# Nine products a job on VectorE, earlier rows of B, and the norm ahead of the gates, in the Mamba layer of a four-layer stack

## The chip, the cores and the metric

The kernel runs on one core of one Trainium2 chip. The metric is the device time of one execution in microseconds (us); smaller is better. Engine names in the profile are PE (TensorE matmul), PEld (TensorE weight load), DVE (VectorE), ACT (ScalarE), POOL (GpSimd) and SP (SyncE, which here issues the DMAs).

## The reference, cut to what matters

Four layers follow each other on a float32 image batch of shape (8, 192, 56, 56), each of the form x + layer(group_norm(x)). Layer 0 is an involution. Layers 1, 2 and 3 are state-space (Mamba) layers. Layer 1, the one that the change is about, cuts the 192 normed channels into three slices of 64 and runs the same Mamba block on each:

```python
xn = layer_norm(group_norm(x))                   # over the 192 channels
for xs in three slices of 64 channels:
    xi, z = xs @ in_proj.T                       # 512 inner channels each
    xc = silu(causal_conv4(xi))
    dt, B, C = split(xc @ x_proj.T)              # 4, 16, 16
    dt = softplus(dt @ dt_proj.T + bias)
    h = h * exp(dt * A) + (dt * xc) * B          # 16 states per channel, along the tokens
    y = (sum over states of h * C) + xc * D
    out = (y * silu(z)) @ out_proj.T + xs
x = x + layer_norm(out of all three) @ proj.T + proj_b
```

Layers 2 and 3 do the same once for all channels, with 384 inner channels.

## The kernel before, in words

**Tiles.** An image has 3136 tokens, cut into 7 chunks of 448 (T). A chunk of layer 1 gives three jobs, one for each slice of 64 channels, called the slice 0, slice 1 and slice 2 job here; 8 images x 7 chunks x 3 slices are 168 jobs. A job has 512 inner channels in nd = 4 groups of 128, and each group has 16 states. A unit treats 4 states of one group: 128 partitions hold 32 channels x 4 states, and the free dimension holds 4 blocks of channels x 448 tokens. So a job of layer 1 has 16 units, numbered 0 to 15, four to a group; q is the number of a unit within its group. Layers 2 and 3 have nd = 3 and 12 units a job.

**What a unit needs.** Line numbers are those of the profile of the kernel before.

- `load_ops` (L713) brings delta and delta times x of a whole group from DRAM, each row repeated for four states, into a tile `rep` (two buffers): four DMAs of 448 KB.
- `decays` (L729): ScalarE takes exp(delta A) into one of two PSUM tiles `da`, one for each half of a unit. Two instructions a half.
- `inputs_begin` (L737): ScalarE copies the carried state into column 0 of the unit's tile `uhg` (nine buffers).
- The product, delta x times B, 128 x 1792 elements. Either GpSimd makes it (`inputs_by_pool`, L748), with B from a row tile that a DMA has spread over the partitions (`row_in`, L629), or VectorE does (`inputs_by_vector`, L754), with B from a PSUM tile `b` that one bfloat16 matmul of TensorE has spread (`spread_b`, L723). There is one `b` bank. The set `pool_units` says which: in layer 1 GpSimd has the eight odd units.
- `scan` (L758): VectorE runs the recurrence, in two halves of 128 x 898. A half needs its decays and the product.
- `keep` (L762): ScalarE copies the last state out. It is the "carry" of the profile.
- `readout` (L767): GpSimd multiplies with C, in place, for every unit, once `keep` is done.
- `reduce` (L773, L776): TensorE sums the states into a PSUM tile `y` (one bank). The first matmul of a group (L773) starts that bank anew and must wait until the group before has been taken out by `gated` (L792), a VectorE product at the head of the units with q = 3.
- `nothing` (L782): matmuls with zeros, which change no result.

**The order is written out by hand.** Engines take their instructions in program order. At unit k the program issues: row loads; `gated`; `reduce(k-3)`; first half of the background; first half `scan(k,0)`; `decays(k+1,0)`; `inputs_begin(k+3)`; GpSimd's product of unit k+2; `readout(k-2)`; VectorE's product of unit k+1; `spread_b(k+2)`; second half of the background; `scan(k,1)`; `keep(k)`; `decays(k+1,1)`.

**The background** prepares the next job while a job runs. It is a list of steps, dealt out by `places` over 32 places (two a unit) in six stretches (`bounds`): convolutions (L1026, evicted at L593); at place 6, that is unit 3, one switch of ScalarE's table for the silus (L596, L577; table back at L569), with the output projection of the job before (L1054, L1056, evicted at L1061); x_proj (L601, evicted at L605), the splitting of B into bfloat16 parts (L612, L613, evicted at L617) and the deltas (L635, evicted at L640); at place 14 (unit 7) or 18 (unit 9) a second switch for the softplus (L643); then delta times x (L647 on TensorE, L650 on VectorE) and its stores; and last the gates (L1044, evicted at L674). A step's cost is a number written at the step. In the slice 0 job the projection and second norm of the chunk before come ahead of the gates. The slice 1 job also holds, behind the gates, the norm of the next chunk: group norm (L330), mean (L537), centring on VectorE (L543), square, variance, scaling (L554), affine (L559), and then eight DMAs (L991) that put the slices into a tile `xs`. The convolutions of the next chunk's first slice read `xs` at the start of the slice 2 job. The softplus switch is at place 14 in the slice 0 job and at place 18 in the other two.

Of the kernel before, what the change touches and what calls it, by code (L numbers as in the profile page):

```python
# [49 lines left out]
def pause(cost=1.0):  # L50
    return Step(None, lambda: None, 9, cost)
# [35 lines left out]
def conv_mamba_stack(ctx: ExitStack, tc: tile.TileContext, a, out):  # L87
# [583 lines left out]
    def evict(w, dst, src, m):  # L671

        if w.inb is None:
            nc.scalar.copy(dst, src)  # L674
        else:
            nc.scalar.activation(dst, src, AF.Identity, bias=w.inb[:, m : m + 1])  # L676

    def gate_steps(pool, w, u, z_mm, z_cost):

        zps = {}  # L680

        def gate(j):
            zps[j] = z_mm(j)

        def gate_out(j):
            if j == 0:
                u.zs = pool.tile([128, w.nd, T], F32, tag="zs", name="zs", bufs=2)
            evict(w, u.zs[:, j, :], zps[j][:, :T], w.nd + j)

        return [Step(lambda j=j: gate(j), lambda j=j: gate_out(j), 1, z_cost) for j in range(w.nd)] + [pause(0.5)]  # L690

    def ssm_layer(pool, w, jobs, n_slots):


        nd = w.nd
        units = [(i, j, q) for i in range(len(jobs)) for j in range(nd) for q in range(NQ)]
        groups = [(i, j) for i in range(len(jobs)) for j in range(nd)]
        per_job = nd * NQ
        pool_units = {1, 3, 5, 7, 9, 11, 13, 15} if nd == 4 else {1, 3, 6, 7, 9, 11}
        pool_rows = sorted({m % NQ for m in pool_units})  # L700
        us = [Layer() for _ in jobs]
        carry = []
        for s in range(n_slots):
# [1 line left out]
        reps, brow, uhg, ys = {}, {}, {}, {}  # L705
# [8 lines left out]
                    out=t[:, r].rearrange("p c t -> p (c t)"), in_=src.unsqueeze(1).to_broadcast([32, 4, 2 * T])  # L714
                )

        def spread_b(k):

            if k in by_pool:
                return  # L720
            i, j, q = units[k]
            brow[k] = banks.b.tile([128, 512], F32, tag="b", name="b")
            nc.tensor.matmul(brow[k][:, :T], lhsT=pick_b[:, q, :], rhs=us[i].parts, start=True, stop=True)  # L723
# [14 lines left out]

        by_pool = {k for k in range(len(units)) if (k % per_job) in pool_units}

        def inputs_by_pool(k):
            if k not in by_pool:
# [5 lines left out]
        def inputs_by_vector(k):  # L750
            if k in by_pool:
                return
            b = brow[k][:, :T].unsqueeze(1).to_broadcast([128, NR, T])
            nc.vector.tensor_mul(uhg[k][:, :, 1:], reps[k // NQ][:, :, 1, :], b)  # L754

        def scan(k, h):
            v = uhg[k][:, 2 * h : 2 * h + 2, :].rearrange("p r t -> p (r t)")
            nc.vector.tensor_tensor_scan(v, banks.da[h][:, 63:961], v, 0.0, ALU.mult, ALU.add)  # L758
# [31 lines left out]
        def gated(g):  # L790
            i, j = groups[g]
            nc.vector.tensor_mul(us[i].zs[:, j, :], us[i].zs[:, j, :], ys[g][:, :T])  # L792

        n_places = 2 * per_job
        def bounds(job):

            silu = 8 if nd == 3 else 6
            softplus = silu + (6 if nd == 3 else 8 if job[0] == 1 else 12)
            return (0, silu), (silu, silu + 2), (silu + 2, softplus), (softplus, softplus + 1), (softplus + 2, softplus + 4), (softplus + 4, n_places)

        def places(*stretches):


# [22 lines left out]
                us[0].row_in(0, q)  # L826
            us[0].row_in(1, q)
        load_ops(0)
        spread_b(0)
        for k in range(3):  # L830
            inputs_begin(k)
        inputs_by_vector(0)
        spread_b(1)
        inputs_by_pool(0)
        inputs_by_pool(1)
        decays(0, 0)
# [2 lines left out]
        n_units = len(units)  # L839
# [7 lines left out]
        for k, (i, j, q) in enumerate(units):  # L847
            m = k % per_job
            if m == 0:

                fetch, outs, rest = tail
                if i + 1 < len(jobs):
                    u = us[i + 1]
                    at = bounds(jobs[i + 1])
                    stretches = *jobs[i + 1][2](u, us[i], outs), rest + jobs[i + 1][3](u)
                    plan = places(*((steps, *p) for steps, p in zip(stretches, at)))
                else:
                    gates = Step(None, lambda: with_gates(lambda: None, us[i]), 0, 0.3, block=True)
                    plan = places(([gates], 4, 6), (outs + rest, 8, n_places))
                plan[3][:0] = [Step(None, fetch, 2, 0.0)]  # L860

            if i + 1 < len(jobs) and m - (per_job - NQ) in pool_rows:
                us[i + 1].row_in(0, m - (per_job - NQ))
            if i and m < NQ:
                us[i].row_in(1, m)
            if k >= NQ + 3 and q == 3:
                gated(k // NQ - 1)
            if k >= 3:
                reduce(k - 3)

            more = 3 - math.ceil(load_of(plan[2 * m] + plan[2 * m + 1]))
            nothing(k - 3, more > 2)
            bg.run(plan[2 * m])
            nothing(k - 3, more > 0)
            load_when_free(k)
            scan(k, 0)
            if k + 1 < n_units:
                decays(k + 1, 0)
            if k + 3 < n_units:
                inputs_begin(k + 3)  # L880
            if k + 2 < n_units:
                inputs_by_pool(k + 2)
            if k >= 2:
                readout(k - 2)
            if k + 1 < n_units:
                inputs_by_vector(k + 1)
            if k + 2 < n_units:
                spread_b(k + 2)
            bg.run(plan[2 * m + 1])
            nothing(k - 3, more > 1)  # L890
            load_when_free(k)
            scan(k, 1)
            keep(k)
            if k + 1 < n_units:
                decays(k + 1, 1)
            if m == per_job - 1:
                tail = jobs[i][4](us[i])
# [67 lines left out]
    def mamba_jobs(pool, w):  # L965
        jobs = []
        chunks = Chunks(pool, 1)
        cks = chunks.all
        for ck in cks:
# [50 lines left out]
            for i in range(3):  # L1020

                def prepare(u, *beside, i=i, ck=ck, norm=norm):
                    def conv_mm(j):
                        pm = mm_tile()
                        for k in range(2):
                            nc.tensor.matmul(  # L1026
                                pm[:, :T], lhsT=w.inconv[:, k, j * 128 : (j + 1) * 128],
                                rhs=ck.xs[:, i, 2 - 2 * k : 2 - 2 * k + T], start=(k == 0), stop=(k == 1),
                            )
                        return pm  # L1030

                    convs, *others, stores = project_steps(pool, w, u, conv_mm, 2, *beside)
                    if i == 0:
                        stores = stores + [Step(None, lambda: chunks.fetch_next(ck), 2)]
                        if ck.place == 0:
                            convs = norm() + convs
                    return convs, *others, stores

                def gates(u, i=i, ck=ck):
                    after_gates = cks[ck.place + 1].norm() if i == 2 and ck.place + 1 < len(cks) else []  # L1040

                    def z_mm(j):
                        pm = mm_tile()
                        nc.tensor.matmul(  # L1044
                            pm[:, :T], lhsT=w.inz[:, j * 128 : (j + 1) * 128], rhs=ck.xs[:64, i, 2 : T + 2], start=True, stop=True
                        )
                        return pm

                    return gate_steps(pool, w, u, z_mm, 1) + after_gates

                def after(u, i=i, ck=ck, finish=finish):
                    def out_proj():
                        u.ps = mm_tile()
                        nc.tensor.matmul(u.ps[:64, :T], lhsT=skip_d, rhs=ck.xs[:64, i, 2 : T + 2], start=True, stop=False)  # L1054
                        for j in range(4):
                            nc.tensor.matmul(u.ps[:64, :T], lhsT=w.outw[:, j, :], rhs=u.zs[:, j, :], start=False, stop=(j == 3))  # L1056

                    def leave():
                        if i == 0:
                            ck.y = pool.tile([64, 3, T], F32, tag="y", name="y")  # L1060
                        nc.scalar.copy(ck.y[:, i, :], u.ps[:64, :T])  # L1061

                    def fetch():
                        if i == 2:
                            chunks.fetch_again(ck)

                    return fetch, [Step(out_proj, leave, 1, 5)], finish() if i == 2 else []

                jobs.append((i, c == 0, prepare, gates, after))
        return jobs  # L1070

# [74 lines left out]
    with ExitStack() as stack:  # L1146
        banks.y = stack.enter_context(tc.tile_pool(name="ps_iy", bufs=1, space=PSUM))
        banks.mm = stack.enter_context(tc.tile_pool(name="ps_im", bufs=6, space=PSUM))
        pool = stack.enter_context(tc.tile_pool(name="inv", bufs=1))
        with tc.manual_schedule():  # L1150
            involution(pool)
    for layer, w in enumerate((w1, w2, w3), 1):
        with ExitStack() as stack:
            scan_banks(stack)
            pool = stack.enter_context(tc.tile_pool(name=f"ssm{layer}", bufs=1))
# [75 lines left out]
```

## Time and profile before

| what | value |
|---|---|
| time, median of 3 runs | 25285.75 us (25262.34 to 25312.53) |
| profiled execution: time and span | 25314.83 us, 25313.0 us |
| share of the span busy: PE, DVE, ACT, POOL | 83%, 89%, 67%, 92% |
| first scan of layer 1, last gating of layer 1 | 1680.36 us, 17363.03 us |
| granted TensorE clock, 2000 to 16000 us | 0.79 of full speed |
| share of DMA engine time, 2000 to 16000 us | 0.36 |

A group of instructions in the profile has its line, engine and operation, what it writes and reads, and its count; behind the first bar stand busy time and mean duration in ns, behind the second the time that the engine was idle just before these instructions, and what it waited for. A line of waits has the waiting engine and line, what it waited for, and total us, times and longest. In a timeline a line has start, duration, engine, line and operation; instructions of one kind that follow each other are merged, and a bracket has the idle time before them with its cause. For TensorE the count of a merged line holds weight loads as well as matmuls.

### The profile page before, as it was taken

What the parts mean: (1) busy time and instruction counts of PE and PEld (TensorE: products, weight loads), DVE (VectorE), ACT (ScalarE), POOL (GpSimd) and SP (SyncE); (2) the same over time, 40 slices, a digit from 0 to 9 for tenths busy, and PEclk for the clock granted to TensorE, in tenths of its full rate; (3) what the DMA queues carried; (4) which work ended last, traced back from release to release, by engine and by line L of the source; (5) the groups of instructions that cost most, each with busy time, mean ns of one, the idle gap of its engine ahead of it and who ended that gap; (6) DMA issues with size and microseconds to landing.
All of it is one profiled execution on the core that took longest, in us unless ns stands there. A gap on an engine that the chain in (4) does not pass through costs nothing.

```text
span 25313.0 us, 232064 instructions
## 1 busy us (share of the span) xinstructions
PE 21123.4 (83%) x71870; PEld 6720.0 (27%) x71870; DVE 22641.3 (89%) x15661; ACT 16946.5 (67%) x32354; POOL 23383.1 (92%) x6772
## 2 busy tenths in 40 slices
PE   9988888888888888888888888888888887888888
PEld 3322222222222222222222222222333332333332
DVE  8879988998899889998998899897999998999998
ACT  1137776767766776766776676676777776777776
POOL 4469999999999999999999999998999998999999
PEclk9988777877777777777777787778888888888888
DMA  4433333333333333333333333333444443444443
GB/s 106 105 101 123 122 119 117 122 121 119 118 122 121 119 120 119 123 119 119 123 119 120 121 120 118 121 119 108 139 141 136 139 140 120 141 138 139 138 145 128
DMA packets 1184872, 3132.61 MB, mean 124 GB/s; under 512 B 163756, under 2 KB 446404, under 8 KB 1183496
## 3 DMA queue, kind: packets, MB, share of 16 engines
q1 hardware_dynamic: 1180824, 3116.70, 37.9%
q8 instruction: 564, 9.24, 0.1%
q14 instruction: 684, 5.60, 0.1%
q10 hardware_dynamic: 2800, 1.06, 0.0%
HBM read 2399.92 MB, written 555.55 MB: 117 GB/s over the span
## 4 chain that ended last, share of the span: by engine, by line
DVE 29%; PE 25%; ACT 19%; issue 11%; POOL 9%; DMA 6%; SPq 2%; DVEq 0%; POOLq 0%; ACTq 0%
DVE uhg L758 20%; ACT da L729 8%; DVE uhg L754 6%; POOL uhg L767 6%; PE y L776 4%; PE mm L635 4%; POOL uhg L748 3%; PE mm L416 3%; DMA rows<-bc 3%; PE y L782 2%; ACT L569 2%; PE y_inv L451 2%; PE y L773 2%; PE mm L612 2%; DMA rep<-ops 2%
## 5 line engine op out<-in xcount | busy, mean ns | idle before, releaser
L758 DVE TENSOR_TENSOR_SCAN uhg<-da,uhg 128x898 f32<-128x898 f32 x8064 | 15928.1, 2011 | 1284.0 <-ACT da L729 1261.9
L767 POOL TENSOR_TENSOR uhg<-uhg,rows 128x1792 f32<-128x1792 f32 x4032 | 14746.3, 3675 | 654.5 <-ACT carry L762 425.9
L729 ACT ACTIVATE da<-rep,k 128x448 f32<-128x448 f32 x16128 | 10255.9, 636 | 1816.6 <-DVE uhg L758 1438.7
L748 POOL TENSOR_TENSOR uhg<-rep,rows 128x1792 f32<-128x1792 f32 x2016 | 8038.2, 3987 | 375.5 <-DMA rep<-ops 206.2
L776 PE MATMUL y<-uhg,k 128*32 128x448 f32 x32256 | 4756.8, 666 | 562.0 <-POOL uhg L767 560.2
L754 DVE TENSOR_TENSOR uhg<-rep,b 128x1792 f32<-128x1792 f32 x2016 | 4031.8, 2000 | 658.9 <-PE b L723 615.1
L762 ACT COPY carry<-uhg 128x4 f32<-128x4 f32 x4032 | 787.3, 195 | 3514.0 <-DVE uhg L758 3464.3
L773 PE MATMUL y<-xc,w_d 128*128 128x448 f32 x2016 | 1522.0, 850 | 1580.5 <-DVE zs L792 1580.3
L782 PE MATMUL y<-w_d,k 128*128 128x448 f32 (+1 forms) x5166 | 2465.1, 586 | 0.0
L1026 PE MATMUL mm<-xs,k 128*128 128x448 f32 x2688 | 1289.7, 617 | 479.6 <-DMA xs<-xg 318.7
L776 PEld LDWEIGHTS y<-uhg,k 128*32 128x32 f32 x32256 | 695.1, 117 | 3664.1 <-issue 2204.0
L1082 PE MATMUL mm<-v,w_in 96*128 96x448 f32 x2688 | 1427.9, 662 | 199.7 <-ACT zs L676 92.4
L635 PE MATMUL mm<-dbl,w_dt 36*128 36x448 f32 (+1 forms) x2016 | 1469.0, 840 | 127.0 <-ACT k L617 127.0
L782 PEld LDWEIGHTS y<-w_d,k 128*128 128x128 f32 x5166 | 1035.4, 215 | 1486.5 <-issue 1459.8
L436 POOL TENSOR_TENSOR x<-x,one 96x448 f32<-96x448 f32 x560 | 633.3, 1135 | 668.3 <-DVE one L428 650.7
L612 PE MATMUL mm<-dbl,k 16*16 16x448 f32 x1120 | 692.7, 707 | 515.7 <-ACT dbl L605 515.7
L428 DVE TENSOR_TENSOR prod<-mm,shifted 128x448 f32<-128x448 f32 x1680 | 932.6, 609 | 207.8 <-PE mm L416 187.3
L1109 PE MATMUL mm<-xin,w_conv 128*128 128x448 f32 x2688 | 1076.4, 543 | 2.0 <-ACT xin L674 1.0
L773 PEld LDWEIGHTS y<-xc,w_d 128*128 128x128 f32 x2016 | 455.0, 265 | 2191.9 <-DVE zs L792 1509.5
L647 PE MATMUL mm<-xc,k 128*128 128x448 f32 x2016 | 983.7, 599 | 31.1 <-DVE dt L650 30.3
L723 PE MATMUL b<-k,k 96*128 96x448 bf16 x2016 | 819.1, 406 | 129.9 <-DVE uhg L754 129.8
L593 ACT ACTIVATE xc<-mm,k 128x448 f32<-128x448 f32 x1008 | 615.3, 627 | 438.9 <-PE mm L1026 327.1
(134 smaller groups left out, 19720.0 us busy)
## 6 DMA issues: line engine op xcount, KB each, us to landing
rep<-ops SPq DMA_DIRECT2D x4032, 448.0 KB, 5.7
ops<-dt SPq DMA_DIRECT2D x1008, 448.0 KB, 3.3
rows<-bc SPq DMA_DIRECT2D x1792, 224.0 KB, 6.2
shifted<-xpad SPq DMA_DIRECT2D x672, 179.0 KB, 4.6
xg<-stream SPq DMA_DIRECT2D x168, 336.0 KB, 3.7
xr<-stream SPq DMA_DIRECT2D x168, 336.0 KB, 5.3
stream<-xr SPq DMA_DIRECT2D x112, 336.0 KB, 3.2
xs<-xg SPq DMA_DIRECT2D x224, 112.0 KB, 6.1
```

Source lines behind the costliest of these rows:

```text
L612: nc.tensor.matmul(u.left[m][:NS, :T], lhsT=ident[:NS, :NS], rhs=u.dbl[:NS, :], start=True, stop=False)
L635: nc.tensor.matmul(u.dps[j][:, :T], lhsT=w.dtw[:, j * 128 : (j + 1) * 128], rhs=u.dbl[:nk, :], start=True, stop=True)
L729: nc.scalar.activation(t[:, 64 + 449 * r : 512 + 449 * r], reps[k // NQ][:, 2 * h + r, 0, :], AF.Exp, scale=w.neg_a[:, j * NR + 2 * h + r, ...
L748: nc.gpsimd.tensor_mul(uhg[k][:, :, 1:], reps[k // NQ][:, :, 1, :], b)
L754: nc.vector.tensor_mul(uhg[k][:, :, 1:], reps[k // NQ][:, :, 1, :], b)
L758: nc.vector.tensor_tensor_scan(v, banks.da[h][:, 63:961], v, 0.0, ALU.mult, ALU.add)
L767: nc.gpsimd.tensor_mul(v, v, us[i].rows[1, q].unsqueeze(1).to_broadcast([128, NR, T]))
L773: nc.tensor.matmul(ys[k // NQ][:, :T], lhsT=w.dd[:, j, :], rhs=us[i].xc[:, j, :], start=True, stop=False)
L776: nc.tensor.matmul(y[32 * r : 32 * r + 32, :T], lhsT=fold, rhs=uhg[k][:, r, 1:], start=False, stop=(q == NQ - 1))
L782: nc.tensor.matmul(ys[k // NQ][:, : nd * 112], lhsT=zeros, rhs=w.dd.rearrange("p j e -> p (j e)")[:, : nd * 112], start=False, stop=False,)
L1026: nc.tensor.matmul(pm[:, :T], lhsT=w.inconv[:, k, j * 128 : (j + 1) * 128], rhs=ck.xs[:, i, 2 - 2 * k : 2 - 2 * k + T], start=(k == 0), st ...
L1082: nc.tensor.matmul(pm[:, :T], lhsT=w.inw[:, k, m * 128 : (m + 1) * 128], rhs=ck.v[:, k, :], start=(k == 0), stop=(k == NCT - 1),)
```

## The change

It has three parts, all in layer 1 (nd = 4).

1. `pool_units` becomes a function. GpSimd makes seven products of a job, not eight: units 1, 3, 6, 7, 10, 12, 14 in the slice 0 job (softplus of the job prepared at place 14), units 1, 3, 6, 8, 9, 12, 14 in the others. VectorE makes nine: 0, 2, 4, 5, 8, 9, 11, 13, 15, or 0, 2, 4, 5, 7, 10, 11, 13, 15. Rows of B are loaded for all four q, not for two.
2. `spread_b` in layer 1 is issued right behind VectorE's product, for the next unit that VectorE multiplies, whichever that is; before, it was issued for unit k+2 in the middle of unit k.
3. The norm of the next chunk stands ahead of the gate steps in their common stretch, not behind them.

```diff
-        pool_units = {1, 3, 5, 7, 9, 11, 13, 15} if nd == 4 else {1, 3, 6, 7, 9, 11}
-        pool_rows = sorted({m % NQ for m in pool_units})
+        def pool_units(i):
+            if nd == 3:
+                return {1, 3, 6, 7, 9, 11}
+            if i + 1 < len(jobs) and bounds(jobs[i + 1])[3][0] < 18:
+                return {1, 3, 6, 7, 10, 12, 14}
+            return {1, 3, 6, 8, 9, 12, 14}
+        pool_rows = (1, 2, 3) if nd == 3 else (0, 1, 2, 3)
...
-        def spread_b(k):
-            if k in by_pool:
+        def spread_b(k=None):
+            if nd == 4:
+                k = by_vector[len(brow)] if k is None and len(brow) < len(by_vector) else None
+            elif k in by_pool:
+                k = None
+            if k is None:
                 return
...
+        by_pool = {i * per_job + m for i in range(len(jobs)) for m in pool_units(i)}
+        by_vector = [k for k in range(len(units)) if k not in by_pool]
...
             nc.vector.tensor_mul(uhg[k][:, :, 1:], reps[k // NQ][:, :, 1, :], b)
+            if nd == 4:
+                spread_b()
...
-            if k + 2 < n_units:
+            if nd == 3 and k + 2 < n_units:
                 spread_b(k + 2)
...
-                    after_gates = cks[ck.place + 1].norm() if i == 2 and ck.place + 1 < len(cks) else []
+                    normed = cks[ck.place + 1].norm() if i == 2 and ck.place + 1 < len(cks) else []
...
-                    return gate_steps(pool, w, u, z_mm, 1) + after_gates
+                    return normed + gate_steps(pool, w, u, z_mm, 1)
```

## The prediction

> **What bounds the kernel now.** I read the groups of instructions first, then a window of pure layer 1 (2000 to 16000 us), then who waited there, then the timelines of VectorE and TensorE over one chunk. Only layer 1 changes. It runs from the first scan at 1680 us to the last gating at 17363 us: 15683 us for 168 jobs, 93.35 us a job, 280 us a chunk.
>
> ```profile
> L758 DVE TENSOR_TENSOR_SCAN uhg<-da,uhg 128x898 f32<-128x898 f32 x8064 | 15928.1, 2011 | 1284.0 <-ACT da L729 1261.9
> L767 POOL TENSOR_TENSOR uhg<-uhg,rows 128x1792 f32<-128x1792 f32 x4032 | 14746.3, 3675 | 654.5 <-ACT carry L762 425.9
> L748 POOL TENSOR_TENSOR uhg<-rep,rows 128x1792 f32<-128x1792 f32 x2016 | 8038.2, 3987 | 375.5 <-DMA rep<-ops 206.2
> L754 DVE TENSOR_TENSOR uhg<-rep,b 128x1792 f32<-128x1792 f32 x2016 | 4031.8, 2000 | 658.9 <-PE b L723 615.1
> ```
>
> One product costs 3.99 us on GpSimd and 2.00 us on VectorE. The window, in the columns PE, PEld, DVE, ACT, POOL busy:
>
> ```profile
> 2000.00:16000.00 14000.00, 11397.85 (x35693) 3323.11 (x35691) 12623.98 (x7640) 9796.58 (x18725) 13444.81 (x3611) 0.79 0.36 120
> ```
>
> GpSimd is 96% busy (89.6 us a job) and VectorE 90% (84.2 us). That invites the reading that GpSimd is the bound. Who waited for whom in this window (total, times, longest) says otherwise:
>
> ```profile
> DVE uhg L758 <- ACT da L729: 640.7, 372, 2.9
> DVE uhg L754 <- PE b L723: 517.9, 249, 5.8
> DVE uhg L758 <- POOL uhg L767: 5.6, 6, 0.9
> ...
> POOL uhg L767 <- ACT carry L762: 347.6, 332, 4.0
> POOL uhg L767 <- DMA rows<-bc: 204.0, 51, 5.1
> ```
>
> VectorE hardly ever waits for GpSimd; GpSimd waits 332 times for a carry, that is for a scan just ended. A scan pair of VectorE sets the pace, together with what ScalarE and TensorE make late for it: some 9 us a job. I place these 9 us in one chunk (8026 to 8306 us), VectorE first:
>
> ```profile
> 8037.24 2.02 DVE L754 TENSOR_TENSOR uhg<-rep,b 128x1792 f32<-128x1792 f32 x1 [5.26 <-PE b L723]
> 8054.18 5.87 DVE L758 TENSOR_TENSOR_SCAN uhg<-da,uhg 128x898 f32<-128x898 f32 x3 [2.85 <-ACT da L729]
> 8083.16 2.02 DVE L754 TENSOR_TENSOR uhg<-rep,b 128x1792 f32<-128x1792 f32 x1 [1.94 <-PE b L723]
> 8287.49 1.08 DVE L543 TENSOR_TENSOR xg<-xg,mm 96x896 f32<-96x896 f32 x1 [1.31 <-ACT carry L762]
> ```
>
> and TensorE beside it:
>
> ```profile
> 8033.50 3.33 PE L1026 MATMUL mm<-xs,k 128*128 128x448 f32 x4 [6.03 <-DMA xs<-xg]
> ...
> 8061.98 1.67 PE L612 MATMUL mm<-dbl,k 16*16 16x448 f32 x2 [4.28 <-ACT dbl L605]
> ...
> 8078.47 1.72 PE L776 MATMUL y<-uhg,k 128*32 128x448 f32 x8
> ...
> 8083.81 0.96 PE L776 MATMUL y<-uhg,k 128*32 128x448 f32 x8
> 8084.70 1.77 PE L647 MATMUL mm<-xc,k 128*128 128x448 f32 x4
> ```
>
> Three sorts of wait: once a chunk TensorE stands for the slices of x (6.03 us), a row of B is queued behind that and VectorE loses 5.26 us; at each silu table switch VectorE loses 2.85 us; and between units 5 and 10 TensorE works without a gap at half pace, so the row of B at 8082.77 is late.
>
> **The change part by part.** All sums are against the profiled execution (25314.83 us, span 25313.0), which lies 29 us above the median of 25285.75; the difference found is then added to the median.
>
> *A. One product more on VectorE.* From a product to the next scan is 1.93 us (8010.38 to 8012.30). 168 jobs x 1.93 = **+324 us** on the path. GpSimd loses 168 x 3.98 = 669 us, of which nothing is on the path by the waits above. Does the product fill a table switch? The one behind silu that could (unit 4's, in the middle of unit 3) is there before and after; the new one (unit 5's) comes after the first scan of unit 4, when the 2.85 us are already over. Units 4 to 6 have no wait for it to fill. The new product of unit 9 or 11 lies after the stall of the softplus switch too. So its price is the whole 1.93 us.
>
> *B. The norm ahead of the gates.* The slices leave in unit 14 instead of at the end of unit 15, one and a half units earlier, about 8 us, against a wait of 6 us; ahead of the convolutions then stand gate matmuls, as in the other two jobs of a chunk, where the same point shows no wait of VectorE. Rows of B cost VectorE 517.9/50 = 10.4 us a chunk; in four chunks read, this first one was 5.26, 4.24, 1.93 and 4.80. I take 4.5 us: 56 x 4.5 = **-252 us** (bounds -110 to -295). SP's queue: eight slice loads (0.53 us each to issue) move ahead of two row loads that are wanted two units later; the queue is free for it. GpSimd's 4 us wait for rows, behind those slices, goes too, off the path.
>
> *C. The norm's first step.* In the new order the mean's matmuls follow the first readout sum of unit 11, and that one waits for the gating at the head of the same unit; VectorE's centring then stands directly behind the first scan of the unit. From a like place in the trace: gating 8275.96, first sum 8276.70 to 8278.36, four readout matmuls to 8280.02, then two mean matmuls of 1.74 us: centring at +6, at full clock at +4.7, where VectorE arrives at +2.5. New wait 2.3 to 3.6 us, taken 3.0, against 1.31 before: 56 x 1.7 = **+95 us** (bounds -73, if the wait just went, to +210).
>
> *D. The other rows of B.* 10.4 - 4.5 = 5.9 us a chunk, 330 us in all, and with the row issued behind the last product they vanish as waits. But they are symptoms of a late TensorE. In the chunk above, the row at 8082.77 is late and 1.94 us are lost; VectorE's next needs are the delta-times-x products, whose operand (L647) ends at 8086.4, and they began at 8087.04. A row in time gains 0.7 us of the 1.94. In the slice 1 job 2.67 us are lost and L647 ends 0.3 us before its use; in the slice 0 job 1.16 us are followed by 0.98 us for the softplus. I take 1.25 us a chunk: **-70 us** (bounds 0 and -330).
>
> *E. What the moved products delay.* Unit 6's product becomes unit 5's and stands before both last scans ahead of the eviction L605, which is queued on ScalarE behind those scans' decays. L605 is what TensorE waits for at 8061.98, and from there the chain of waits runs through TensorE to L650. So x-dependent work comes 1.9 us later in the slice 0 and slice 2 jobs and 0.3 us in the slice 1 job, where it hangs on L617: 4.1 us a chunk, 230 us, if TensorE is as slow as now; nothing, if it isn't. Here a rule speaks. The Trainium skill (TensorE: Matmul & The Clock Gate, Part 1) says that the array falls to half clock after an idle window of about 3.4 us and is at full clock again after about 3.4 us of sustained work. The trace agrees with the fall (after 4.28 us idle four readout matmuls take 1.72 us, not 0.96) but not with the return: at 8078.47, after 16 us without a gap, they still take 1.72. By the rule the stretch to 8084.70 would be some 9 us shorter and E would be 0; by the row E is 230. The new waits break long idle gaps into shorter ones, so I take half: **+115 us**.
>
> *F. TensorE waits for VectorE.* A row's matmul now waits for the product just issued, and everything behind it on TensorE too: output projection (unit 3), gates (unit 15), and the last matmul L647 (units 8 or 10). The first two are evicted a unit later, so the cover holds. The last is wanted at once: row 0.36 + matmul 0.9 + hand-overs 0.3 - the other 0.5 us product between = 0.6 to 1.1 us, in two of three jobs. 112 x 0.6 = **+67 us** (bounds 0 and +125).
>
> *G. More on GpSimd's side.* Two more row loads a job (224 KB each, DMA engines 36% busy) are issued three units ahead of their product: 0. Units 8 and 12, first of their groups, are now multiplied on GpSimd, which wants their rep tile earlier: for unit 12, loaded at the head of unit 7 (some 2.7 us of issue, 5.7 us to landing), at about the time that it lands. A wait of 1 us there would stay on GpSimd: 0.
>
> Sum: 324 - 252 + 95 - 70 + 115 + 67 = +279 us: 25286 + 279 = about **25560 us**.
>
> **Rivals.**
> 1. *TensorE keeps its clock* (ends faster). Thirteen shorter waits a job replace the 3 to 8 us gaps; if the stretch of units 5 to 10 runs at full clock, as it does in some slice 2 jobs (at 5257.65 the same stretch costs VectorE 0.65 us instead of 3.26), all of D counts, and the 1.3 us waits for decays in unit 8 go. 324 - 252 - 330 - 75 + 56 + 67 = -210: about 25080 us. It decides as soon as the readout sums of units 6 to 8 take 0.96 us. Against it: the low matmuls (16 and 36 rows) of this stretch stay, and the slice 0 job turned slow after a gap of only 1.79 us. Chance 0.20.
> 2. *GpSimd was the bound* after all; then VectorE's 84.2 + 1.9 us and the waits left over (some 4 us) remain, 90 us a job, 168 x 3.35 = 563 us less: about 24720 us. Against it, the waits. Chance 0.02.
> 3. *A wash*: B larger and E nil, within 0.2%, which is about what a measurement of this kernel can tell from no change: 25235 to 25336. Chance 0.10.
> 4. *Half clock from unit 3 on*: the gap before the row in unit 3 makes the output projection slow (5.1 us instead of 3.2, as at 8231.96), TensorE reaches L612 some 2 us late in every job: 168 x 2 = 336 us more, about 25900. Chance 0.12.
> 5. *The sum above*: chance 0.56.
>
> **How the numbers follow.** Faster 0.22 (rivals 1 and 2), same 0.10, slower 0.68. The range runs from rival 1 to most of rival 4: 25090 to 25830.
>
> **What would show it.** A: VectorE's products rise from 2016 to 2184, and GpSimd in layer 1 falls to some 90%, without a gain. B: no wait for the slices. C: centring waits for PE by 2 to 4 us. D: rows of B gone from VectorE's waits. E, F: L650 waits for L647, and VectorE's waits for decays no smaller. TensorE's clock over layer 1 above 0.83, or VectorE's waits under 7 us a job, would prove me wrong.

## The result and the profile after

| kernel | median, us | ratio to before, 95% interval |
|---|---|---|
| before (4 runs beside the changed kernel) | 25287.67 | |
| changed kernel | 25665.42 (25655.08 to 25684.17) | 1.015 [1.0133, 1.0168] |

The change costs 378 us; the forecast was +279 us (the span rose from 25313.0 to 25682.1 us, +369). Layer 1 now runs from 1683.34 to 17728.64 us, 95.5 us a job instead of 93.35. First the groups of the changed kernel that answer to the four of before. The columns are the same; the order is scan, readout, GpSimd's product, VectorE's product:

```profile
L781 DVE TENSOR_TENSOR_SCAN uhg<-da,uhg 128x898 f32<-128x898 f32 x8064 | 15927.8, 2009 | 1425.3 <-ACT da L741 1416.7
L790 POOL TENSOR_TENSOR uhg<-uhg,rows 128x1792 f32<-128x1792 f32 x4032 | 14756.8, 3674 | 1614.9 <-ACT carry L785 1578.4
L769 POOL TENSOR_TENSOR uhg<-rep,rows 128x1792 f32<-128x1792 f32 x1848 | 7369.1, 3988 | 422.9 <-DMA rep<-ops 212.6
L775 DVE TENSOR_TENSOR uhg<-rep,b 128x1792 f32<-128x1792 f32 x2184 | 4353.2, 1993 | 96.4 <-PE b L735 50.5
```

One product of each job has changed its engine (2016 to 2184 on VectorE, 2016 to 1848 on GpSimd), at unchanged durations. GpSimd's busy time fell by 669 us on its products, and its idle time ahead of the readouts rose from 654.5 to 1614.9 us. The window of pure layer 1, then VectorE's waits in it, then TensorE's:

```profile
2000.00:16000.00 14000.00, 11341.75 (x35083) 3275.88 (x35083) 12626.63 (x7614) 9538.92 (x18291) 12577.41 (x3380) 0.78 0.36 122
```

```profile
DVE uhg L781 <- ACT da L741: 767.7, 427, 3.3
DVE xg L543 <- PE mm L537: 197.2, 49, 5.0
DVE y L554 <- ACT mm L550: 88.5, 42, 2.1
DVE dt L650 <- PE mm L647: 82.7, 106, 1.6
DVE zs L815 <- PE y L799: 66.7, 80, 1.2
```

```profile
PE b L735 <- DVE uhg L775: 1429.5, 599, 7.6
PE y L796 <- DVE zs L815: 828.1, 348, 3.3
```

TensorE's first row as it was before:

```profile
PE b L723 <- DVE uhg L754: 93.1, 43, 2.7
```

VectorE's 517.9 us of waits for rows of B are gone, and so is every wait for the slices of x. But VectorE is as busy as it was (12626.63 against 12623.98 us) while it gets through fewer jobs of the window, each with one product more. So it waits as long in all: adding up all its waits of the window gives 1370 us before and 1362 us now, which is 9.1 and 9.3 us a job. What the norm's new place saves, other waits have taken. And TensorE now stands 599 times, 1429.5 us, for a product of VectorE (93.1 us before). What is behind that row in TensorE's queue is late.

One chunk shows how, at two places of it (start, duration and so on, as in the timelines of before). VectorE:

```profile
8064.51 1.54 DVE L554 TENSOR_TENSOR y<-y,mm 64x1344 f32<-64x1344 f32 x1 [2.10 <-ACT mm L550]
...
8155.48 0.59 DVE L815 TENSOR_TENSOR zs<-zs,y 128x448 f32<-128x448 f32 x1
8155.99 2.02 DVE L781 TENSOR_TENSOR_SCAN uhg<-da,uhg 128x898 f32<-128x898 f32 x1
8161.77 1.08 DVE L543 TENSOR_TENSOR xg<-xg,mm 96x896 f32<-96x896 f32 x1 [3.75 <-PE mm L537]
```

and TensorE at the same two places:

```profile
8047.11 2.47 PE L537 MATMUL mm<-y,k 64*64 64x448 f32 x6
...
8058.07 0.55 PE L735 MATMUL b<-k,k 96*128 96x448 bf16 x1 [7.60 <-DVE uhg L775]
8058.56 4.74 PE L537 MATMUL mm<-sq,k 64*64 64x448 f32 x6
...
8156.22 1.83 PE L796 MATMUL y<-xc,w_d 128*128 128x448 f32 x2 [3.25 <-DVE zs L815]
8157.98 1.72 PE L799 MATMUL y<-uhg,k 128*32 128x448 f32 x8
8159.63 2.09 PE L537 MATMUL mm<-xg,k 96*96 96x448 f32 x4
```

The last three rows of each, after the gating of unit 11 in the slice 1 job, are the prediction's step C as it was put: gating, first sum (L796), readout matmuls at half pace, mean (L537), centring 6.3 us after the gating. The rows ahead of them are what the prediction did not list. At 8050.47 TensorE reached the row of B for the next product, and stood 7.60 us for the product before it. Behind it in the queue were the mean-of-squares matmuls of the second layer norm. They ended at 8063.30, ScalarE evicted them (L549, L550), and VectorE stood 2.10 us for them at L554. Two things made them late. They started behind the stall, and they took 4.74 us where the same number of matmuls had taken 2.47 us ahead of it (8047.11). The granted clock, the third column from the end, shows the difference:

```profile
8040.00:8050.40 10.40, 7.71 (x37) 2.19 (x29) 8.54 (x6) 5.29 (x12) 8.81 (x3) 1.00 0.71 268
8058.00:8067.00 9.00, 8.93 (x18) 2.34 (x19) 6.90 (x6) 3.79 (x8) 7.71 (x3) 0.50 0.44 137
```

At the pace of before the stall they would have ended about 2.3 us sooner (4.74 less 2.47), about as much as VectorE stood. The half pace alone does not cost that: in a chunk with parts 1 and 3 the same matmuls took 4.74 us as well (at 7986.90), but ended ahead of the gating and nobody waited for them. Here they start late and then run at half clock, and the wait takes both.

### The profile page after: what moved, and what is told of

It is laid out like the page before. It is cut to its first block, busy times and chain, and to the rows that moved or that the text cites. A ratio compares the mean times of both kernels' runs of the same rounds, so it can differ in the third digit from the quotient of the medians.

```text
span 25682.1 us, 233041 instructions
## 1 busy us (share of the span) xinstructions
PE 21364.4 (83%) x72148; PEld 6757.0 (26%) x72148; DVE 22976.4 (89%) x15829; ACT 16909.6 (66%) x32354; POOL 22745.6 (89%) x6604
## 4 chain that ended last, share of the span: by engine, by line
DVE 37%; PE 23%; ACT 19%; issue 11%; DMA 5%; POOL 4%; SPq 1%; DVEq 0%; ACTq 0%; POOLq 0%
DVE uhg L781 25%; DVE uhg L775 10%; ACT da L741 8%; PE mm L635 4%; PE y L799 3%; PE mm L416 3%; POOL uhg L790 3%; DMA rep<-ops 3%; ACT L569 2%; DMA rows<-bc 2%; PE mm L612 2%; PE y_inv L451 2%; POOL uhg L769 1%; ACT zs L577 1%; ACT dt L643 1%
## 5 line engine op out<-in xcount | busy, mean ns | idle before, releaser
L790 POOL TENSOR_TENSOR uhg<-uhg,rows 128x1792 f32<-128x1792 f32 x4032 | 14756.8, 3674 | 1614.9 <-ACT carry L785 1578.4
L769 POOL TENSOR_TENSOR uhg<-rep,rows 128x1792 f32<-128x1792 f32 x1848 | 7369.1, 3988 | 422.9 <-DMA rep<-ops 212.6
L775 DVE TENSOR_TENSOR uhg<-rep,b 128x1792 f32<-128x1792 f32 x2184 | 4353.2, 1993 | 96.4 <-PE b L735 50.5
L796 PE MATMUL y<-xc,w_d 128*128 128x448 f32 x2016 | 1561.6, 871 | 1174.1 <-DVE zs L815 1170.4
L735 PE MATMUL b<-k,k 96*128 96x448 bf16 x2184 | 878.9, 402 | 1668.0 <-DVE uhg L775 1666.9
L1043 PE MATMUL mm<-xs,k 128*128 128x448 f32 x2688 | 1223.2, 585 | 77.9 <-ACT zs L674 61.8
L796 PEld LDWEIGHTS y<-xc,w_d 128*128 128x128 f32 x2016 | 456.1, 270 | 2129.6 <-DVE zs L815 1289.3
L647 PE MATMUL mm<-xc,k 128*128 128x448 f32 x2016 | 965.9, 589 | 34.6 <-DVE dt L650 33.8
L1061 PE MATMUL mm<-xs,k 64*128 64x448 f32 x1344 | 942.4, 809 | 23.6 <-ACT zs L674 15.9
```

What stands on the lines that cost most here:

```text
L769: nc.gpsimd.tensor_mul(uhg[k][:, :, 1:], reps[k // NQ][:, :, 1, :], b)
L790: nc.gpsimd.tensor_mul(v, v, us[i].rows[1, q].unsqueeze(1).to_broadcast([128, NR, T]))
L796: nc.tensor.matmul(ys[k // NQ][:, :T], lhsT=w.dd[:, j, :], rhs=us[i].xc[:, j, :], start=True, stop=False)
L1043: nc.tensor.matmul(pm[:, :T], lhsT=w.inconv[:, k, j * 128 : (j + 1) * 128], rhs=ck.xs[:, i, 2 - 2 * k : 2 - 2 * k + T], start=(k == 0), st ...
```

## The experiments

The three parts were first run one by one and in pairs. "Part" has the numbers of the section on the change; differences in us are the ratio less one, times 25287.67 us, and their intervals reach some 30 us to either side. The theory in all of them is that the added product costs VectorE's own time, and that a row issued at once makes TensorE stand for the product ahead of it. The rivals are that what GpSimd is relieved of decides, or TensorE's clock.

**Part 3 alone.**

```diff
-                    return gate_steps(pool, w, u, z_mm, 1) + after_gates
+                    return normed + gate_steps(pool, w, u, z_mm, 1)
```

> The kernel before with part 3 alone: the norm ahead of the gates. Theory 1 (VectorE with what TensorE and ScalarE make late for it is the bound; step B gives back the wait for the slices, step C costs a wait at the centring): B -250 us, C +125 us (4.0 us of waiting for the mean in the changed kernel against 1.8 before, 56 chunks), so 25290 - 125 = about 25165 us. Rival (the loss of the changed kernel comes from the norm's new place): slower than before, 25400 us or more.

Measured: 25015.85 us, 0.9889 [0.9876, 0.9903], -281 us. VectorE's waits in the window, and the centring in the chunk shown above:

```profile
DVE uhg L758 <- ACT da L729: 666.4, 370, 2.8
DVE uhg L754 <- PE b L723: 312.8, 200, 2.7
DVE xg L543 <- PE mm L537: 84.1, 51, 2.7
```

```profile
8152.32 1.99 DVE L754 TENSOR_TENSOR uhg<-rep,b 128x1792 f32<-128x1792 f32 x1
8155.81 1.08 DVE L543 TENSOR_TENSOR xg<-xg,mm 96x896 f32<-96x896 f32 x1 [1.49 <-PE mm L537]
```

Rows of B: 517.9 to 312.8 us. The centring waits for TensorE now, but no longer than before (84.1 against 88.5 us for L543). VectorE makes the product of unit 12 just ahead of it. In the changed kernel that product is GpSimd's, and the centring waits 3.75 us.

**Part 2 alone** (rows right behind the product, eight products).

```diff
             nc.vector.tensor_mul(uhg[k][:, :, 1:], reps[k // NQ][:, :, 1, :], b)
+            if nd == 4:
+                spread_b()
...
-            if k + 2 < n_units:
+            if nd == 3 and k + 2 < n_units:
                 spread_b(k + 2)
```

> The kernel before with part 2 alone: the row of B issued right behind VectorE's product, still eight products. Theory 1: the waits for rows that are not the slices' (330 us) vanish, most of them come back as waits for delta times x and decays, and TensorE's waits for VectorE cost some 70 us: within 100 us of before, 25190 to 25390. Rival (the loss comes from TensorE waiting for VectorE's product): slower by 300 us or more, about 25600.

Measured: 25375.43 us, 1.0029 [1.0018, 1.004], +73 us. No wait for rows is left, and the sum of VectorE's waits in the window is 1378 us against 1370: decays took 200 us more, the centring 129, L650 102, the gating 65.

**Part 1 alone** (nine products; rows for unit k+2 and the norm where they were).

```diff
-        pool_units = {1, 3, 5, 7, 9, 11, 13, 15} if nd == 4 else {1, 3, 6, 7, 9, 11}
+            if i + 1 < len(jobs) and bounds(jobs[i + 1])[3][0] < 18:
+                return {1, 3, 6, 7, 10, 12, 14}
+            return {1, 3, 6, 8, 9, 12, 14}
```

> The kernel before with part 1 alone: nine products on VectorE, rows of B issued as before, norm behind the gates. Theory 1: 324 us for the products and 100 to 200 us because L605 comes later: 25290 + 450 = about 25740 us, slower than the full change. Rival (GpSimd was the bound): faster than before, 25000 us or less.

Measured: 25608.43 us, 1.012 [1.0106, 1.0134], +303 us. The sum of VectorE's waits is 1327 us, or 9.0 us a job where it was 9.1: the price is the product's own time, step A's 324 us. TensorE's wait for products grew without part 2 too:

```profile
PE b L731 <- DVE uhg L771: 675.3, 293, 4.1
```

The new sets put units of VectorE's next to each other (4 and 5, 8 and 9 or 10 and 11, and 15 with the next job's 0). There the old order already issues a row right behind a product. So not all of the changed kernel's 1429.5 us comes from part 2, and VectorE's waits a job stayed as they were beside 675.3 us of standing: TensorE's standing by itself is no measure of the cost.

**Parts 1 and 2, and parts 1 and 3.** Each is the changed kernel with the third part taken back.

> The changed kernel with the norm put back behind the gates (parts 1 and 2). Theory 1: the change without B's gain and C's cost, 25665 + 125 = about 25790 us. If parts 1 and 2 are each what costs and the norm helps nothing: about 25665. Rival (the norm's new place is the loss): 25400 or less.

> Parts 1 and 3: norm ahead, nine products, rows of B issued as before. In the run with the norm alone GpSimd is 98% busy. Theory 1 (VectorE is the bound even there): the price of part 1 alone, 304 us, comes on top of 25016: about 25320 us. Rival (with the slices' wait gone GpSimd has become the bound, so its relief pays): 25150 us or less.

Measured: 25777.78 us, 1.0187 [1.0173, 1.02], +473 us; and 25498.83 us, 1.0075 [1.0062, 1.0088], +190 us. With parts 1 and 3 TensorE stands 935.9 us for products. **Parts 2 and 3**, with eight products:

> Parts 2 and 3 with eight products: norm ahead, row of B right behind the product. Against part 3 with the rows half a unit later (24969 us) it differs in step F alone, TensorE's wait for the product. If F costs what the wait forces on what stands behind (theory 1, revised): 80 to 150 us more, 25050 to 25120. If it is the early row itself that costs in the runs with part 2: 24970.

Measured: 24997.35 us, 0.9886 [0.9871, 0.99], -288 us. The seven combinations:

| parts | 1 | 2 | 3 | 1+2 | 1+3 | 2+3 | 1+2+3 |
|---|---|---|---|---|---|---|---|
| us to before | +303 | +73 | -281 | +473 | +190 | -288 | +379 |

One by one the parts add up to +95 us, together they cost +379. Part 3 is worth 281 us with eight products and 113 with nine (303 to 190). Part 2 costs 73 us alone, nothing beside part 3, and 170 and 189 us with nine products.

**More work for GpSimd.** In the changed kernel GpSimd makes unit 6's product twice in every job, writing the same values.

```diff
+            for _ in range(2 if nd == 4 and k % per_job == 6 else 1):
                 nc.gpsimd.tensor_mul(...)
```

> The changed kernel, in which GpSimd makes the product of unit 6 twice in every job of layer 1 (the same values are written again): its relief is taken back, 168 x 3.99 = 670 us of work, VectorE's ninth product stays. Theory 1 (nothing of GpSimd's relief was on the path): within 50 us of the changed kernel, 25620 to 25720. Rival (the relief was worth something that the other costs hid): slower by what it was worth, 25900 us or more.

Measured: 25690.23 us, 1.015 [1.0137, 1.0164], the changed kernel's ratio. GpSimd's wait for carries shrank from 1365.2 us to this, and nothing else moved:

```profile
POOL uhg L791 <- ACT carry L786: 809.0, 462, 5.8
```

So 669 us of GpSimd's time are worth 25 us of the kernel's by the medians and nothing by the ratios, with some 30 us of uncertainty in each.

**Part 2 alone, with zero matmuls to keep TensorE busy.** Two matmuls with zeros ahead of each row.

```diff
             if nd == 4:
+                nothing(k - 4, 2)
                 spread_b()
```

> Part 2 alone (25375 us), with two matmuls with zeros put on TensorE ahead of every early row of B, in the time in which it waits for VectorE's product. If part 2 costs through TensorE's clock (0.79 before, 0.77 with part 2 over 2000 to 16000 us), the fillers bring the clock to 0.85 or more and the time falls, to 25250 or less. If it costs through the order alone (matmuls behind the row come later), the fillers bring nothing or add up to 100 us: 25375 to 25480.

Measured: 25415.41 us, 1.003 [1.002, 1.004]; part 2 alone had 1.0029. The profiled execution is one of its quickest (25287.92 us), so its rows are no average. Its window:

```profile
2000.00:16000.00 14000.00, 12167.45 (x40564) 3988.05 (x40563) 12686.95 (x7657) 9824.14 (x18762) 13472.49 (x3617) 0.88 0.36 121
```

The granted clock is 0.88 against 0.77, and the median is no lower. But the zero matmuls take TensorE's time as well (VectorE's waits for readout sums at the gating rose from 72.6 to 202.9 us), so this shows that fillers bring no net gain here, not what a higher clock alone is worth. Within its 22 runs the quick ones have the higher clock over the whole span (25260.58 us at 0.885, 25462.11 us at 0.877), so the clock may well be worth something; whether it is cause or companion is not shown.

**Unit 12's product back on VectorE** in the slice 1 job, parts 1 and 3, to cover the centring as in part 3 alone.

```diff
+            if i + 1 < len(jobs) and jobs[i + 1][0] == 2:
+                return {1, 3, 6, 8, 9, 13, 14}
```

> Parts 1 and 3 (25499 us), with unit 12 given back to VectorE and unit 13 to GpSimd in the slice 1 job only, so that a product of VectorE stands between the first scan of unit 11 and the centring, as in the run with the norm alone. If the centring waits in the run with parts 1 and 3 because that product was moved away (3.5 us a chunk against 1.7 with the norm alone): 60 to 110 us faster, 25390 to 25440. If the wait has another cause: 25499.

Measured: 25640.36 us, 1.0143 [1.0126, 1.016], against 1.0075 for parts 1 and 3 (0.7% worse). VectorE's waits in the window:

```profile
DVE uhg L773 <- PE b L733: 346.3, 209, 2.7
DVE xg L543 <- PE mm L537: 138.6, 49, 3.1
DVE dt L650 <- PE mm L647: 60.9, 49, 1.6
```

The centring's wait fell from 176.8 to 138.6 us, but rows of B rose from 223.5 to 346.3, and L650 now waits for L647. This set also puts three units of VectorE's in a row (10, 11, 12). My theory that the lost cover at the centring is what nine products cost part 3 fell: covering it this way moves the wait.

**The ninth product added with the even ones kept**: unit 9 or 11 joins units 0, 2, ... 14, and units 4 to 6 stay as they were.

```diff
-                return {1, 3, 6, 7, 10, 12, 14}
-            return {1, 3, 6, 8, 9, 12, 14}
+                return {1, 3, 5, 7, 11, 13, 15}
+            return {1, 3, 5, 7, 9, 13, 15}
```

> Part 1 in another choice of units: the eight even units stay with VectorE, and unit 9 (slice 0 job) or 11 is added, so that no product is moved ahead of L605's scans. Step E says that the choice of unit 5 in place of 6 costs 115 to 230 us: then 25390 to 25490, against 25608 with part 1 alone. If step E is nil: the same as that run within 40 us.

Measured: 25715.91 us, 1.0171 [1.0156, 1.0186], slower than part 1 alone (1.012 [1.0106, 1.0134]). Step E's saving did not come. The two sets differ in the late units as well, and this one too has three in a row (8 to 10, or 10 to 12), so it doesn't measure unit 5 against unit 6 by itself.

**Part 3 with rows half a unit later.** Eight products; the row for the next product is issued behind the second half of the background, not right behind the product.

```diff
             bg.run(plan[2 * m + 1])
+            if nd == 4 and k + 1 < n_units and k + 1 not in by_pool:
+                spread_b()
```

> Part 3, and part 2 in another place: the row of B for VectorE's next product is issued behind the second half of the unit's background, half a unit after the product, so that TensorE need not wait for it; eight products. Theory 1: the 313 us of waits for rows (2000 to 16000 us) that part 3 alone leaves go, most come back as waits for delta times x and decays, and no wait of TensorE is added: 24900 to 25000 us. Rival (an early row costs wherever it stands, since the waits for it are all symptoms and cover others): 25016 us or more.

Measured: 24969.24 us, 0.9866 [0.9853, 0.9879], the lowest median of all, 1.3% ahead of before. Against parts 2 and 3 (0.9886 [0.9871, 0.99]) only the row's place differs. TensorE's wait for products is half as long (745.8 us with parts 2 and 3, then this):

```profile
PE b L735 <- DVE uhg L775: 372.2, 154, 3.8
```

But the time differs by 28 us in the medians and the intervals overlap, so with eight products a gain from the later row is not clear of noise. With nine products a later row was not run. The same, with two gate steps ahead of the norm:

> Part 3 with the rows half a unit later (24969 us), and two of the four gates put ahead of the norm, so that the mean's matmuls no longer follow the first readout sum of unit 11 at once. The centring waits 3.1 us a chunk there. Theory 1: half to all of it goes, 80 to 170 us: 24800 to 24890 us. If the slices come late again or the wait only moves: 24969 or more.

Measured: 25014.41 us, 0.9895 [0.9879, 0.9911]: the centring waits less (128.5 against 153.2 us), L650 more, and nothing is gained. VectorE's waits in the fastest kernel:

```profile
DVE uhg L779 <- ACT da L741: 648.3, 410, 2.8
DVE xg L543 <- PE mm L537: 153.2, 51, 3.1
DVE zs L813 <- PE y L797: 68.9, 95, 0.9
```

No row is waited for, and decays stand where they stood before (648.3 against 640.7 us). All its waits in the window come to 1038 us, against 1370 before and 1135 with part 3 alone.

## Why the prediction was right, and where it was not

The sign and the bound were right: VectorE sets the pace, and a product moved to it is paid in full. The size, +379 against +279, comes out of three errors that partly cancel, and that it came this near is in part luck. Putting the parts on in the order 1, 3, 2, the prediction had +439 (A and E), -157 (B and C) and -3 (D and F); the runs have +303, -113 and +189.

- **A, +324: right.** Part 1 alone costs 303 us with VectorE's waits a job all but unchanged (9.0 us for 9.1), and handing 669 us back to GpSimd changes nothing that these runs can tell. The new product fills no table switch: at 8210.82 the first scan of unit 4 still waits 2.84 us, and the new product follows it.
- **B, -252: right.** The four readings that the prediction gives average 4.1 us a chunk; it took 4.5 and gave no reason. With part 3 alone rows of B save 205 us in the window of 50 chunks, with nine products 234 (457.6 to 223.5): 230 to 268 us over 56 chunks.
- **C, +95: right in kind for the changed kernel, but too small.** The centring waits 197.2/49 = 4.0 us a chunk, beyond the 2.3 to 3.6 us that were forecast; before it was 88.5/50 = 1.8 us, not 1.31. That makes 56 x 2.25 = +126 us. It is not the price of part 3, though: with part 3 alone the wait is 84.1/51 = 1.6 us, no more than before.
- **E, +115: failed.** "Unit 6's product becomes unit 5's and stands before both last scans ahead of the eviction L605", and so later work "comes 1.9 us later": part 1 alone makes that move and costs 21 us less than A. The set that keeps units 4 to 6 as they were was slower still. The row that stood against the rule was read correctly: before, from 8062 to 8078.4 us, TensorE is busy 16.40 of 16.40 us and its granted clock is 0.50. But the wait at the end of E's chain did not grow (L650's waits in the window are 41 us with part 1 alone, 56 before). How much later L605 itself came was not measured. "The new waits break long idle gaps into shorter ones" was wrong as well: TensorE's new waits are up to 7.6 us long, and the granted clock in the window went from 0.79 to 0.78.
- **D and F, -3: failed in size, at F.** F charged one operation behind the waiting row, "the last matmul L647", at 0.6 us in two of three jobs: +67 us, at most +125. The runs have +189 for D and F together. L650's waits did appear (56 to 171 us in the window), but the row also holds up the layer norm's matmuls (L554, 88 us, where there was no wait; L543, 23 us) and what leads to ScalarE's decays (669 to 768 us when part 2 joins parts 1 and 3). In that step the sum of VectorE's waits rises by 135 us in the window (1227 to 1362), which is an estimated 155 us over layer 1, although 224 us of waits for rows vanish; the two profiled spans differ by 160. The granted clock in the window is 0.78 in both, so the mean clock does not tell them apart. So D's symptoms did vanish as named, and returned elsewhere.
- **G, 0: right.** Waits of VectorE for rep tiles stay at some tens of us.

Not settled: why each set of nine products changes the waits as it does. The even ones plus one (part 1 alone) and unit 12 for 13 (parts 1 and 3) made TensorE later for rows or for L647; that the order of TensorE's queue does it is argued from the waits, not shown by a run. The wait at L554 stands only where parts 1 and 2 meet (88.8 us with the two, 88.5 with all three, 1.2 with part 1 alone, none with part 2 alone), so it is one piece of what the pair costs beyond its sum. How part 2 delays the decays on ScalarE was not followed instruction by instruction. The effects of pairs (for example -80 us for parts 2 and 3 beyond their sum) carry some 50 us of uncertainty each.

## What to carry to other kernels

Ask of an engine's busy share who waits for it: GpSimd was 96% busy, and 669 us less of its work were worth at most some tens of us, as its work hung on VectorE's scans. On an in-order queue, an instruction that is issued at the first moment it can be wanted becomes a stop for everything behind it; list every consumer behind it before calling such a wait cheap. Half a unit later the stop was half as long here; what that is worth in time is not shown. Test the parts of a bundled change alone: here one was worth 1.1%, and the other two hid it.

## What the runs showed of the hardware

From kernel to kernel the mean granted clock said little about the time: part 1 alone ran at 0.80 in the window and cost 303 us, the fastest kernel at 0.76. At single places it did count: behind the 7.60 us stall the matmuls of the layer norm ran at a granted clock of 0.50 and took 4.74 us instead of 2.47. The time from issue to landing of the same eight slice loads depended on where they were issued: the median was 6.1 us before, and 2.2 us in the changed kernel (2000 to 16000 us). In the chunks read, the slices of before were issued 3.1 us behind four loads of 448 KB (8021.43 and 8024.52), those of the changed kernel 21 us behind such loads (8157.07 and 8178.32).
